# Four graph layers on one core: where the second chunk of layer 2 is fetched to, and where the pieces of layer 3 stand between the pairs

## The chip, the cores and the metric

The kernel runs on one core of a Trainium2 chip. A core has a matrix engine (TensorE, "PE" in the profile, with a row "PEld" for its weight loads), a vector engine (DVE), a scalar engine (ACT), GpSimd (POOL) and a sync engine (SP), which here only issues DMAs. The engines run side by side; each works off its own queue in order, and semaphores hold an instruction until what it needs is there. Matmuls write to PSUM, everything else lies in SBUF, and 16 DMA engines bring data from HBM.

The metric is device time in microseconds of one execution. Before the change, three executions took 528.18, 528.65 and 530.54 us; the median is 528.65.

## The reference

There are N = 3327 nodes with 64 features and a sparse N x N adjacency matrix. Four layers follow each other, each inside a residual with a layer norm:

```python
x = _layernorm(x + _L0_gnn_ref(x, adj, L0_gnn_W), axis=-1)
x = _layernorm(x + _L1_gnn_ref(x, adj, L1_gnn_weight, L1_gnn_bias), axis=-1)
x = _layernorm(x + _L2_gnn_ref(x, adj, L2_gnn_W, L2_gnn_b), axis=-1)
x = _layernorm(x + _L3_gnn_ref(x, adj, L3_gnn_weight, L3_gnn_bias), axis=-1)
```

The change concerns the last two. Layer 2 takes the sum over neighbours and a small dense step:

```python
h_neigh = (adj @ X + X) / deg
z = concat([X, h_neigh]) @ W + b
out = relu(z);  out / max(norm(out), 1e-12)
```

Layer 3 does not use the values of the adjacency but the place of each neighbour in its row, counted from the end, and weighs the last hundred with powers of one half:

```python
mask = (adj != 0)
rank = cumsum(mask, axis=1)
pos = rank - (deg - min(deg, 100))
w = mask * where(pos > 0, 0.5 ** (min(deg, 100) - pos), 0)
out = w @ (input @ weight) + bias
```

## The kernel before

**Tiling.** The nodes are padded to 3328 = 26 blocks of 128. The adjacency, transposed, is cut into 4 chunks of 832 target nodes (`CH`), and each chunk into 13 pairs of source blocks; one pair is 128 partitions x 2 x 832 fp32 (832 KB) and is fetched by `load_adj` (line 276) as one DMA, or as two when its target is a list of two tiles (line 281; the whole form is line 285). All these DMAs are issued by SP, in order.

**Layer 2** runs over the chunks in the order `ORDER2` = 2, 3, 1, 0. I call these pass 1 to pass 4. For a pair, `aggregate_pair` (line 442) issues four matmuls that add to the chunk's PSUM bank; the profile shows each as two instructions, so a pair is eight matmuls of line 448. After the last pair, `keep_sums` (line 432) copies the bank to SBUF in two halves (DVE or ACT, line 435), `prologue2` (line 1189, after the eleventh pair) has transposed the chunk's own features (line 1196), and `epilogue2` (line 1211) does the dense step and the norm: two matmul instructions per block on line 1218, then a chain on DVE, ACT and POOL from line 1224 to line 1259. Near its end the new features are split into three bf16 parts, high, middle and low (lines 1254 to 1257, tile `parts`), which layer 3 uses. The epilogue of pass 1 is issued behind the first pair of pass 2; that of pass 2 behind pass 2, and so on.

**Pass 2 also finds ranks.** The chunk 3 (`LATE_RANKS`) is the only one whose ranks are not yet known from layer 0. For each pair DVE makes a mask (line 474, or line 470 twice when the pair lies in two tiles), PE counts with twelve matmuls (`count`, line 520), DVE carries the count over to the next mask (`carry`, line 506), and ACT writes the ranks from PSUM to SBUF (line 530). The counts of a pair follow two pairs later (`LATE_LAG`). The ranks go to `last_rank`, which is the same memory as `uw`. The halves of `uw`, called `ut` and `wt`, are two operands of layer 1 that are no longer needed; each again has two halves, which hold one pair each. The one row of ranks that needs a correction is handled by `last_rows` (line 536) with small DMAs on POOL's queue and three DVE instructions (lines 548 to 550).

**Where pairs lie.** Most pairs go through four buffers (`adjp`). Since layer 1 needs them too, the first nine pairs of pass 1 are fetched during layer 1's end into memory that is free then (`load_ahead2`, line 1156): both halves of wt, both halves of ut (one of them twice) and eight tiles of layer 1 that hold half a pair each. The last four pairs of pass 1 are still in the four buffers from layer 1. Pairs 12 and 11 of pass 2, which come first there, go into four tiles of a pool with ten buffers (tag `m16`, line 1186), which the masks and the expanded ranks use as well:

```python
ahead = [
    load_adj(
        ORDER2[1], jp, [mp.tile([P, CH], FP, name="a1", tag="m16") for _ in range(2)]
    )
    for jp in (NB // 2 - 1, NB // 2 - 2)
]
```

**Layer 3** is cut into 52 pieces, one per pair and chunk. A piece needs the ranks of its pair and chunk, which `expand` (line 1265) turns into bf16 powers of two, nine pieces ahead, on DVE (line 1279) or ACT (line 1277), and the parts of the pair's two blocks. It is then twelve matmuls of line 1302 into a PSUM bank of its chunk. The four banks lie where the counts of pass 2 had theirs. Which part of `parts` exists when: pass 1's epilogue makes blocks 13 to 18, pass 2's 19 to 25. So a piece of pair 9 (blocks 18 and 19) and all of pairs 10 and 11 need pass 2's epilogue.

Twelve pieces (pairs 7, 8, 9) are issued in pass 3, one behind each pair from the second on; eight (pairs 10 and 11) in pass 4, one behind each pair from the first on; 32 after layer 2. In pass 3 the three pieces of chunk 3 come last (`sorted`, line 1351), since their ranks are the latest.

**The order.** The program is written with a framework that orders each engine's instructions itself, in the order of the program where it sees no reason against it. `issue_after(a, b)` (line 148) draws an edge without a semaphore: a stands behind b in the queue of their engine. In pass 2 every pair is pinned behind the counts before it in this way; in passes 3 and 4 neither pairs nor pieces are pinned, so their matmuls can be mixed.

Of the kernel before, what the change touches and what calls it, by code (L numbers as in the profile page):

```python
# [20 lines left out]
FP = mybir.dt.float32  # L21
# [10 lines left out]
P = 128  # L32
NB = 26
NP = NB * P
D = 64
CH = 832
# [6 lines left out]
ORDER2 = (2, 3, 1, 0)  # L43
# [67 lines left out]
def four_gnn_layers_kernel(  # L111
# [14 lines left out]
    nc = tc.nc  # L126
# [305 lines left out]
    def keep_sums(c, acc, row, both=False):  # L432

        for h in range(2):
            (nc.vector.tensor_copy if both and h == 0 else nc.scalar.copy)(
                sums[row : row + D, bass.ds(c * CH + h * HC, HC)], acc[h * D : (h + 1) * D, 0:HC]
            )

    def halves(t):
        return t.rearrange("p (h c) -> p h c", h=2)  # L440
# [200 lines left out]
    with ExitStack() as l0s:  # L641
# [3 lines left out]
        places = Places(banks)  # L645
# [507 lines left out]

    def load_ahead2(more):

        def load(k, t):  # L1160
            return load_adj(ORDER2[0], PAIRS[k], t)

        def view(t, k):
            return t[:, bass.ts(k, 2 * CH)].rearrange("p (b i) -> p b i", b=2)

        loaded = [load(k, view(*t)) for k, t in enumerate(((ut, 0), (wt, 0), (wt, 1)))]
        yield loaded
        places = [[more(2 * i + k) for k in range(2)] for i in range(4)]
        loaded += [load(3 + k, t) for k, t in enumerate((*places, view(ut, 1)))]
        yield  # L1170
        loaded.append(load(8, view(ut, 0)))

    def begin2(banks, loading, loaded, behind):

# [8 lines left out]
    def layers_2_and_3(banks, acc, done, there):  # L1183


        with tc.tile_pool(name="l2m", bufs=10) as mp, tc.tile_pool(name="late", bufs=1) as late:
# [24 lines left out]
            def epilogue2(c, x2, behind=None):  # L1211


                b0, b1_, nb = blocks_of(c, GROUPS2)
                work, alone = Work(nb), c == ORDER2[-1]
                pb = per_block(banks.pair(2), nb, 2 * D)
                for k in range(nb):
                    issued = nc.tensor.matmul(
                        pb[:, k, :], lhsT=sums[:, bass.ts(b0 + k, P)], rhs=wl2, start=True, stop=True
                    )  # L1220
                    if behind is not None:
                        issue_after(issued, behind)
                y = node_tile("y2")[:, 0:nb, :]
                nc.vector.tensor_tensor(y, pb[:, :, D : 2 * D], col(scale2[:, b0:b1_], nb), op=ALU.mult)
                nc.vector.tensor_tensor(y, y, pb[:, :, 0:D], op=ALU.add)
                nc.vector.tensor_scalar_max(y, y, 0.0)
                ss = work("ss")
                sum_of_squares(y, nb, ss, alone)

                m = small.tile([P, GB], FP, name="ln_m", tag="ln_m")  # L1230
                nc.vector.tensor_reduce(m[:, 0:nb], y, axis=AX.X, op=ALU.add)
                nc.vector.tensor_scalar(m[:, 0:nb], m[:, 0:nb], 1.0 / D, None, op0=ALU.mult)
                aside = nc.vector if alone else nc.gpsimd
                aside.tensor_tensor(y, y, col(m, nb), op=ALU.subtract)
                nc.vector.tensor_scalar_max(ss, ss, 1e-24)
                r, k = (rsqrt(ss, work), 1.0) if alone else (table_norm(ss, work), 0.375)
                nc.vector.scalar_tensor_tensor(y, y, k, col(r, nb), op0=ALU.mult, op1=ALU.mult)
                aside.tensor_add(y, y, x2)
                ss = work("ss")
                sum_of_squares(y, nb, ss, alone)  # L1240
                r, k = (deviation(ss, work), 1.0) if alone else (table_root(ss, work), -0.5 / D)
                left = node_tile("left")
                copy = nc.vector.tensor_copy if alone else nc.scalar.copy

                for k0, k1 in ((0, 3), (3, nb)) if alone else ((0, nb),):
                    xs = x3[:, b0 + k0 : b0 + k1, :]
                    first = nc.vector.scalar_tensor_tensor(
                        xs, y[:, k0:k1, :], k, col(r[:, k0:k1], k1 - k0), op0=ALU.mult, op1=ALU.mult
                    )
                    if k0 > 0:  # L1250
                        issue_after(first, issued)

                    hi, mid, lo = (parts[:, b0 + k0 : b0 + k1, bass.ts(i, D)] for i in range(3))
                    copy(hi, xs)
                    nc.vector.tensor_sub(left[:, k0:k1, :], xs, hi)
                    nc.vector.tensor_copy(mid, left[:, k0:k1, :])
                    issued = nc.vector.tensor_sub(lo, left[:, k0:k1, :], mid)
                xs = x3[:, b0:b1_, :]
                aside.tensor_tensor(
                    xs, xs, bias["b3"].to_broadcast([P, nb, D]), op=ALU.add  # L1260
                )

            acc3, begun, bits_of, ranks_of = {}, set(), {}, {}

# [16 lines left out]
                    issue_after(issued, behind)  # L1281
                return issued

            def piece(k):
                last = None
                if not acc3:

# [11 lines left out]
                for b in range(2):  # L1299
                    for part in range(3):  # L1300
                        for h in range(2):
# [4 lines left out]
                                start=(c not in begun and b == 0 and part == 0),  # L1306
                                stop=(last and b == 1 and part == 2),
                            )
                begun.add(c)
                return issued  # L1310

            def epilogue3(b0, b1_, bank, behind):
# [29 lines left out]
                if full < b1_:  # L1342
# [4 lines left out]

            early = {2: (7, 8, 9), 3: (10, 11)}
            pieces = [(c, jp) for jps in (*early.values(), (12, 4, 5, 6)) for jp in jps for c in ORDER2]
            behind = 4 * len(early[2])  # L1350
            pieces[0:behind] = sorted(pieces[0:behind], key=lambda piece: piece[0] == LATE_RANKS)
            pieces += [(c, jp) for c in ORDER2 for jp in (0, 1, 2, LAST_PAIR)]
            left3 = len(pieces) - 4 * NCH
            beside = range(left3 - L3_LEFT + BITS_AHEAD, left3 - L3_LEFT + BITS_AHEAD + L3_BESIDE)

            ahead = [
                load_adj(
                    ORDER2[1], jp, [mp.tile([P, CH], FP, name="a1", tag="m16") for _ in range(2)]
                )
                for jp in (NB // 2 - 1, NB // 2 - 2)  # L1360
            ]
            rows = last_rows(late, [(c, rank[:, c]) for c in ORDER2 if c != LATE_RANKS])
            next(rows)
            k = 0
            for n, c in enumerate(ORDER2):
                if n > 0:
                    acc = banks.one(n % 2)
# [7 lines left out]
                for i, jp in enumerate(order):  # L1375
                    if n == 0 and i < EARLY:
                        continue
                    if n == 0 and jp in there:
                        a2 = there.pop(jp)
                    elif n == 1 and i < 2:  # L1380
                        a2 = ahead.pop(0)
                    else:
                        a2 = load_adj(c, jp)
                    issued = aggregate_pair(acc, xr, a2, jp, i == 0, i == NB // 2 - 1, counted)
                    if n == 1 and i == 0:
                        epilogue2(ORDER2[0], x2, issued)
                    if ranks:
                        mask = ranks.mask(jp, a2)
                        counted = count(masked, places, min(LATE_LAG, jp), issued)
                    if i == OWN2_AT:  # L1390
                        x2, made = prologue2(c, issued)
                        if n == 0:
                            step(rows, made)
                            all_of(rows)
                    if n in early and 0 <= i - 3 + n < 4 * len(early[n]):
                        piece(k)
                        k += 1
                if ranks:
                    late_rows = last_rows(late, [(c, last_rank)])
                    next(late_rows)  # L1400
                keep_sums(c, acc, D, n > 0)

                if n > 0:
                    epilogue2(c, x2)
            while k < left3:
                piece(k)
                k += 1
# [73 lines left out]
```

## Time and profile before

| what | us |
|---|---|
| median of three executions | 528.65 |
| profiled execution, whole | 529.18 |
| its span in the profile | 527.5 |
| layers 0 and 1 and the change to layer 2, to the first pair of pass 1 | 349.8 |
| pass 1, to the first pair of pass 2 | 19.2 |
| pass 2, to the first pair of pass 3 | 36.2 |
| pass 3, to the first pair of pass 4 | 42.1 |
| pass 4, to the end of its epilogue's matmuls | 31.4 |
| the rest of layer 3 and the output | 48.9 |

The stages begin with the first line 448 matmul of the pass in PE's timeline (349.81, 368.95, 405.15, 447.22), and pass 4 ends with line 1218 at 478.60; the passes overlap, so the first pairs of pass 3 run between the last counts of pass 2.

In the profile every row is a group of instructions: the line, the engine, the operation, the tile that is written and those that are read. A bracket at the end of a timeline row gives how long the engine was idle just before, and what ended the wait. Matmuls overlap, so a row's duration is longer than its share of PE's time; the distance from start to start is what counts. A stretch row gives the busy time of each engine between two moments, the clock that PE was granted (1.00 is full), and the load on the DMA engines.

### The profile page before, as it was taken

What the parts mean: (1) busy time and instruction counts of PE and PEld (TensorE: products, weight loads), DVE (VectorE), ACT (ScalarE), POOL (GpSimd) and SP (SyncE); (2) the same over time, 40 slices, a digit from 0 to 9 for tenths busy, and PEclk for the clock granted to TensorE, in tenths of its full rate; (3) what the DMA queues carried; (4) which work ended last, traced back from release to release, by engine and by line L of the source; (5) the groups of instructions that cost most, each with busy time, mean ns of one, the idle gap of its engine ahead of it and who ended that gap; (6) DMA issues with size and microseconds to landing.
All of it is one profiled execution on the core that took longest, in us unless ns stands there. A gap on an engine that the chain in (4) does not pass through costs nothing.

```text
span 527.5 us, 8494 instructions
## 1 busy us (share of the span) xinstructions
PE 481.2 (91%) x3256; PEld 238.7 (45%) x3256; DVE 386.5 (73%) x704; ACT 334.9 (63%) x394; POOL 177.2 (34%) x150
## 2 busy tenths in 40 slices
PE   5999898999967999999998999899899998999993
PEld 3555343454432333533343344354444664656672
DVE  3565438979669978799789968976888973726844
ACT  1445544776868999879978896711477653316931
POOL 2001101212007788867876795503202120200000
PEclk9999999999999999999999999999999999999998
DMA  8899999989438687767767786397997796880012
GB/s 270 309 357 344 390 341 388 334 274 316 190 113 336 201 267 254 255 197 254 262 195 238 232 277 232 135 386 240 342 317 270 272 341 260 294 290 2 1 23 50
DMA packets 46179, 132.52 MB, mean 251 GB/s; under 512 B 6934, under 2 KB 7038, under 8 KB 46066
## 3 DMA queue, kind: packets, MB, share of 16 engines
q1 hardware_dynamic: 45602, 131.35, 72.3%
q0 software_dynamic: 384, 0.52, 0.4%
q8 instruction: 27, 0.44, 0.3%
q14 instruction: 22, 0.18, 0.1%
q10 hardware_dynamic: 144, 0.03, 0.0%
HBM read 130.86 MB, written 0.85 MB: 250 GB/s over the span
## 4 chain that ended last, share of the span: by engine, by line
PE 50%; DVE 23%; DMA 11%; ACT 10%; issue 3%; POOL 1%; DVEq 0%; ACTq 0%; POOLq 0%
PE one L448 13%; DMA adj<-in_adjt_dram 11%; PE two L1302 10%; DVE p L828 7%; PE two L817 6%; PE one L848 6%; PE two L520 5%; DVE mask L506 4%; PE two L448 4%; ACT s L841 3%; DVE s L836 3%; DVE mask L474 3%; ACT s L842 2%; ACT rank L530 2%; PE one L1317 1%
## 5 line engine op out<-in xcount | busy, mean ns | idle before, releaser
L843 POOL TENSOR_TENSOR s<-s,p 128x832 f32<-128x832 f32 x67 | 130.0, 1954 | 71.5 <-ACT s L842 59.5
L828 DVE SCALAR_TENSOR_TENSOR p<-two,adj 128x832 f32<-128x832 f32 x100 | 101.0, 1018 | 17.9 <-issue 13.4
L817 PE MATMUL two<-uw 64*128 64x416 f32 x416 | 88.5, 537 | 14.7 <-DVE s L836 7.1
L530 ACT ACTIVATE rank<-two,last_bias 128x832 uint8<-128x832 f32 x78 | 71.7, 952 | 46.3 <-PE two L520 24.3
L448 PE MATMUL one<-adj,x0w 128*64 128x416 f32 x416 | 82.6, 524 | 4.1 <-DMA adj<-in_adjt_dram 2.6
L848 PE MATMUL one<-s,xu 128*64 128x416 f32 x416 | 85.2, 524 | 0.0
L841 ACT ACTIVATE s<-two,far_bias 128x832 f32<-128x832 f32 x67 | 63.6, 950 | 21.9 <-DVE p L828 19.9
L506 DVE SCALAR_TENSOR_TENSOR mask<-two,minus_last,mask 32x832 bf16<-32x832 f32 x48 | 52.5, 1093 | 27.5 <-PE two L520 23.3
L448 PE MATMUL one<-adj,xr 128*64 128x416 f32 x296 | 69.7, 515 | 2.2 <-DMA adj<-in_adjt_dram 2.1
L1302 PE MATMUL two<-bits,parts 128*64 128x416 bf16 x624 | 69.0, 340 | 0.0
L817 PEld LDWEIGHTS two<-uw 64*128 64x128 f32 x416 | 36.8, 185 | 66.6 <-PE one L848 22.6
L474 DVE TENSOR_SCALAR mask<-adj 128x1664 bf16<-128x1664 f32 x50 | 52.7, 1055 | 15.5 <-DMA adj<-in_adjt_dram 14.6
L842 ACT ACTIVATE s<-s 128x832 f32<-128x832 f32 x67 | 60.1, 897 | 1.9
L520 PE MATMUL two<-mask,tri 128*64 128x416 bf16 x416 | 50.6, 345 | 10.1 <-DVE mask L506 7.6
L1302 PEld LDWEIGHTS <-parts 128*64 128x64 bf16 x624 | 40.2, 110 | 21.3 <-issue 3.4
L848 PEld LDWEIGHTS one<-s,xu 128*64 128x64 f32 x416 | 25.8, 136 | 47.5 <-issue 46.6
L448 PEld LDWEIGHTS one<-adj,x0w 128*64 128x64 f32 x416 | 29.2, 138 | 36.4 <-issue 23.4
L520 PEld LDWEIGHTS <-tri 128*64 128x64 bf16 x416 | 23.9, 110 | 44.2 <-issue 25.1
L836 DVE SCALAR_TENSOR_TENSOR s<-two,p 128x832 f32<-128x832 f32 x37 | 37.6, 1016 | 2.9 <-ACT two L833 2.4
L448 PEld LDWEIGHTS one<-adj,xr 128*64 128x64 f32 x296 | 27.1, 137 | 22.7 <-issue 14.7
L833 ACT ACTIVATE two<-two,far_bias 128x832 f32<-128x832 f32 x37 | 34.0, 918 | 4.9 <-DVE p L828 4.7
L1277 ACT ACTIVATE bits<-rank 128x1664 uint16<-128x1664 uint8 x21 | 32.3, 1579 | 5.6 <-PE two L1302 5.6
(265 smaller groups left out, 453.9 us busy)
## 6 DMA issues: line engine op xcount, KB each, us to landing
adj<-in_adjt_dram SPq DMA_DIRECT2D x139, 832.0 KB, 4.9
uw<-in_adjt_dram SPq DMA_DIRECT2D x5, 832.0 KB, 5.9
sums<-in_adjt_dram SPq DMA_DIRECT2D x2, 832.0 KB, 6.0
p<-in_adjt_dram SPq DMA_DIRECT2D x4, 416.0 KB, 5.1
s<-in_adjt_dram SPq DMA_DIRECT2D x4, 416.0 KB, 7.3
a<-in_adjt_dram SPq DMA_DIRECT2D x4, 416.0 KB, 4.0
uw<-in_xt_dram SPq DMA_DIRECT2D x1, 640.0 KB, 11.2
out_dram<-o SPq DMA_DIRECT2D x3, 192.0 KB, 2.5
```

Of the source, the lines that this page charges most:

```text
L448: issued = nc.tensor.matmul(acc[h * D : (h + 1) * D, 0:HC], lhsT=x[:, 2 * jp + k, 0:D], rhs=a[:, bass.ts(h, HC)], start=(first and k == 1) ...
L474: issued = nc.vector.tensor_scalar(mask, a2, 0.0, None, op0=ALU.not_equal)
L506: ranks.carried = nc.vector.scalar_tensor_tensor(halves(last), ranks.after[P - 32 : P, :, 0:HC], minus_last[P - 32 : P, :], halves(last), ...
L520: issued = nc.tensor.matmul(counts[k][rows, h, 0:HC], lhsT=lhsT[:, rows], rhs=mask[:, of, bass.ts(h, HC)], start=lhsT is tri, stop=(k == 1 ...
L530: nc.scalar.activation(halves(ranks.rank[:, 2 * jp + k, :]), counts[k][:, :, 0:HC], AF.Relu, bias=last_bias,)
L817: issued = nc.tensor.matmul(v[:, h, 0:HC], lhsT=wt[rows, bass.ts(jb, P)], rhs=ut[rows, bass.ds(c * CH + h * HC, HC)], start=True, stop=True,)
L828: issued = nc.vector.scalar_tensor_tensor(halves(p), v, 0.25 - 0.5 * FD, halves(a), op0=ALU.add, op1=ALU.mult)
L841: nc.scalar.activation(halves(s), v, AF.Square, bias=far_bias, scale=-2.0)
L842: nc.scalar.activation(s, s, AF.Copy, bias=FG)
L843: nc.gpsimd.tensor_mul(s, s, p)
L848: issued = nc.tensor.matmul(acc[h * D : (h + 1) * D, 0:HC], lhsT=xu[:, jb, 0:D], rhs=s[:, bass.ts(h, HC)], start=first, stop=last,)
L1302: issued = nc.tensor.matmul(acc3[c][h * D : (h + 1) * D, 0:HC], lhsT=parts[:, 2 * jp + b, bass.ts(part, D)], rhs=bits[:, b, bass.ts(h, HC) ...
```

## The change

Four things change, all in layers 2 and 3; no instruction is added or removed.

- Pass 2's first four pairs are now all fetched ahead. Pairs 12 and 11 go into the two halves of wt, pairs 10 and 9 into the four `m16` tiles. The other nine go through the four buffers.
- Each piece that is issued in passes 3 and 4 is pinned: its matmuls stand behind the last matmul of the pair before it, and the next pair's matmuls stand behind the piece.
- The sort covers all 20 pieces of passes 3 and 4 rather than the first 12. So the five pieces of chunk 3 come last of all, in pass 4, and three pieces of pair 10 move from pass 4 to pass 3.
- The first copy of a pass's sums (`keep_sums`, on DVE) stands behind the last parts instruction of the epilogue before it.

```diff
@@ keep_sums
         for h in range(2):
-            (nc.vector.tensor_copy if both and h == 0 else nc.scalar.copy)(
+            issued = (nc.vector.tensor_copy if both and h == 0 else nc.scalar.copy)(
                 sums[row : row + D, bass.ds(c * CH + h * HC, HC)], acc[h * D : (h + 1) * D, 0:HC]
             )
+            if h == 0:
+                first = issued
+        return first
...
+    def half_of(t, k):
+        return t[:, bass.ts(k, 2 * CH)].rearrange("p (b i) -> p b i", b=2)
...
@@ piece
-            def piece(k):
+            def piece(k, behind=None):
...
+                            if behind is not None:
+                                issue_after(issued, behind)
...
@@ layers_2_and_3
             early = {2: (7, 8, 9), 3: (10, 11)}
-            behind = 4 * len(early[2])
+            behind = 4 * sum(map(len, early.values()))
             pieces[0:behind] = sorted(pieces[0:behind], key=lambda piece: piece[0] == LATE_RANKS)
...
-            ahead = [
-                load_adj(
-                    ORDER2[1], jp, [mp.tile([P, CH], FP, name="a1", tag="m16") for _ in range(2)]
-                )
-                for jp in (NB // 2 - 1, NB // 2 - 2)
+            ahead = [half_of(wt, k) for k in range(2)] + [
+                [mp.tile([P, CH], FP, name="a1", tag="m16") for _ in range(2)] for _ in range(2)
             ]
+            ahead = [load_adj(ORDER2[1], NB // 2 - 1 - k, t) for k, t in enumerate(ahead)]
...
-                    elif n == 1 and i < 2:
+                    elif n == 1 and ahead:
                         a2 = ahead.pop(0)
...
                     if n == 1 and i == 0:
-                        epilogue2(ORDER2[0], x2, issued)
+                        made = epilogue2(ORDER2[0], x2, issued)
...
                     if n in early and 0 <= i - 3 + n < 4 * len(early[n]):
-                        piece(k)
+                        counted = piece(k, issued)
                         k += 1
...
-                keep_sums(c, acc, D, n > 0)
+                copied = keep_sums(c, acc, D, n > 0)
+                if made is not None and n > 0:
+                    issue_after(copied, made)

                 if n > 0:
-                    epilogue2(c, x2)
+                    made = epilogue2(c, x2)
```

## The prediction

> **What bounds the kernel now.** I read the page first, then the chain of waits, then a table of stretches, and last the timelines of PE, DVE and SP around the places where the chain leaves PE. "Pass 1" to "pass 4" are layer 2's four chunks in their order 2, 3, 1, 0. From the page and the chain in order of time:
>
> ```profile
> PE 481.2 (91%) x3256; PEld 238.7 (45%) x3256; DVE 386.5 (73%) x704; ACT 334.9 (63%) x394; POOL 177.2 (34%) x150
> ...
> 385.57 1.06 PE two L520 x12
> 386.63 1.40 PE one L448 x8
> ...
> 478.60 22.80 PE two L1302 x257
> ```
>
> PE is busy 91% of the span, and the chain gives clean prices: one pair of layer 2 (line 448) costs 1.40 us, the counts of one pair (line 520) 1.06, a matmul of layer 3 (line 1302) 22.80/257 = 0.0887, so a piece of twelve 1.065. Shares cannot tell what the change is worth; these stretches can (columns: PE, PEld, DVE, ACT, POOL busy, PE's granted clock, DMA share, GB/s):
>
> ```profile
> 357.00:360.00 3.00, 3.00 (x22) 1.16 (x17) 2.17 (x7) 0.54 (x1) 0.06 (x1) 1.00 0.32 121
> 368.95:405.15 36.20, 33.26 (x249) 16.68 (x247) 31.35 (x47) 23.65 (x29) 6.38 (x9) 1.00 0.95 326
> 377.80:380.05 2.25, 0.00 (x0) 0.00 (x0) 2.17 (x5) 1.99 (x4) 1.15 (x2) 1.00 0.97 163
> 415.49:449.05 33.56, 31.85 (x254) 18.97 (x255) 21.57 (x40) 14.01 (x15) 5.73 (x5) 1.00 0.77 277
> 444.00:449.00 5.00, 5.00 (x48) 3.13 (x43) 3.24 (x6) 3.25 (x3) 0.00 (x0) 1.00 0.06 22
> ```
>
> The DMA engines are nearly idle twice: at 357 to 360, where SP has nothing that it may issue, and at 444 to 449, where all four buffers are full and PE does not free one. Pass 2 (368.95 to about 405) loses PE time. PE, and then DVE:
>
> ```profile
> 377.28 0.52 PE L520 MATMUL two<-mask,tri 128*64 128x416 bf16 x4
> 380.05 0.54 PE L520 MATMUL two<-mask,tri 128*64 128x416 bf16 x4 [2.25 <-DVE mask L506]
> ...
> 383.28 0.54 PE L520 MATMUL two<-mask,tri 128*64 128x416 bf16 x4 [0.59 <-DVE mask L506]
> ```
> ```profile
> 374.22 1.03 DVE L474 TENSOR_SCALAR mask<-adj 128x1664 bf16<-128x1664 f32 x1 [0.74 <-DMA adj<-in_adjt_dram]
> ...
> 377.19 1.02 DVE L474 TENSOR_SCALAR mask<-adj 128x1664 bf16<-128x1664 f32 x1
> ...
> 378.91 1.09 DVE L506 SCALAR_TENSOR_TENSOR mask<-two,minus_last,mask 32x832 bf16<-32x832 f32 x1
> 380.40 1.03 DVE L474 TENSOR_SCALAR mask<-adj 128x1664 bf16<-128x1664 f32 x1 [0.41 <-DMA adj<-in_adjt_dram]
> ```
>
> PE waits 2.25 and 0.59 us for the carry (line 506), which stands in DVE's queue behind masks whose pairs landed late. Pass 3 ends like this:
>
> ```profile
> 439.61 0.56 PE L448 MATMUL one<-adj,xr 128*64 128x416 f32 x1 [1.22 <-DMA adj<-in_adjt_dram]
> ...
> 441.22 4.76 PE L1302 MATMUL two<-bits,parts 128*64 128x416 bf16 x52
> ```
> ```profile
> 432.83 0.61 DVE L1256 CAST parts<-left 128x448 bf16<-128x448 f32 x1
> 438.44 0.58 DVE L435 COPY sums<-one 64x416 f32<-64x416 f32 x1 [5.00 <-PE one L448]
> 439.06 0.62 DVE L1257 TENSOR_TENSOR parts<-left,parts 128x448 bf16<-128x448 f32 x1
> ```
>
> Pairs without pieces outran the DMA (0.30, 0.19 and 1.22 us of waits), then 52 piece matmuls ran in one block before pass 4's pairs, which is when the DMA idled. They needed the parts of line 1257, which DVE did only after a copy that waits for the pass's end.
>
> **The first edit: four pairs ahead.** Pairs 12 and 11 of pass 2 go to the two halves of wt, pairs 10 and 9 to the four tiles that held 12 and 11. Issues stay 15 (2 whole, 4 halves, 9 whole, against 4 halves and 11 whole), each 0.37 us of SP's free time. Before, SP stood here:
>
> ```profile
> SPq L281 <- PE two L448: 4.6, 1, 4.6
> ```
>
> until 359.90. The halves of wt come free when pass 1's pairs 1 and 2 are done (352.83 and 354.23), so the two loads can go at about 352.9 and 354.3, ahead of the halves that still wait. At the 406 GB/s of 352 to 356 they are 4.2 us of DMA work, of which the idle stretch takes about 3. Each later pair of pass 2 then has two pairs fewer ahead of it: the load behind the 0.41 us gap landed at 380.38 and would land near 375.
>
> Gain: the carry at 378.91 has in front of it the 0.74 us gap and the 1.02 us mask, both of which move ahead, so it starts 1.76 us earlier; its input (counts that ended at 376.05) allows that. The 0.59 us wait goes too, since the gap and mask before it at 380.40 move ahead. 1.76 + 0.59 = 2.35 us. Ends: 2.84 (both waits whole), and nothing, or up to 1.5 us lost, if DVE's line 548, which waits for POOL's small loads issued at 360.67 to 363.85 (6.6 and 7.0 us to land), is pushed back by the deeper DMA backlog; all masks queue behind it. I take 2.35. What is late next in pass 2 is PE itself: pair and counts are 2.46 us, DVE's mask and carry 2.12, a loaded pair 2.41 (852 kB at the 353 GB/s of 388 to 392).
>
> **The second edit: pins and order, costed together.** Pass 3's first two pairs stay free; from its third on, every pair stands behind a piece. That takes from PE the pairs which filled the end of pass 2's counts (1.75 pairs, 405.15 to 415.49 had no idle). I count from the counts' last matmul (412.40) to pass 4's second pair (449.05): 36.65 us before. After, the last counts start 0.4 earlier (their carry ended at 411.09; a pair held PE until 411.53): 412.0. Behind it stand epilogue2 twice (1.80 as at 476.80, and 1.61 as at 370.44), 13 pieces (13.85), 12 pairs (16.80), one prologue (0.85): 34.9 us, so 446.9, which is 2.15 less than 449.05, plus new waits:
>
> - The first piece needs the PSUM pairs that the counts used. ACT empties them by 415.13, while PE is through epilogue2 at 413.8: 1.35 us at most; ACT does 1.58 us of bits in between, without which it is nothing. I take the middle, 0.65.
> - The seventh piece (pair 9) is the first to need the second chunk's parts. PE gets to its second half at 413.8 + 0.65 + six pieces 6.4 + six pairs 8.4 + 0.5 = 429.8. The parts end 24.1 us after epilogue2's matmuls before (415.56 to 439.68), 18.5 without the copy in front (the new edge between copy and epilogue excludes it), and 16.2 if also the late ranks' bits are gone from that stretch (0.46 + 1.02 us at 427.41, 0.74 on ACT at 429.57, 0.5 at 430.86; they move to pass 4). So 432.3 or 430.0: a wait of 2.5 or 0.2. I take 0.5, nearer the second, since those bits do move.
>
> Moving the late pieces behind all others changes no count (20 pieces in passes 3 and 4, 32 after); pass 4 runs a piece behind each of its first eight pairs either way, and its tail stays paced by loads that wait for a buffer. At 2.465 us for pair and piece against 2.41 for a load, DMA keeps up; if it moved only the 326 GB/s of pass 2's row (2.61 us a pair), eleven pairs would cost 1.6 us more. The edge between copy and epilogue in pass 2 changes nothing: the copy stood at 408.94, the epilogue's end at 407.14.
>
> [...] Where PE stood idle 2.25 us at 377.80, the granted clock stayed 1.00. [...]
>
> **Sum.** -2.35 - 2.15 + 0.65 + 0.50 = -3.35 us. The profiled execution took 529.18 (span 527.5), 0.53 above the median 528.65. On the execution 525.83, on the median 525.3. A measurement tells about 0.5%, 2.6 us, from no change.
>
> **Rivals.**
> - *Both waits vanish.* -2.84 - 2.15, and the 0.7 us that PE idles at 402.3 to 403.3 for the first epilogue's DVE work: -5.7, 522.95. For it: pass 2's inputs land 5 us early. Against: DVE is 31.35 of 36.20 us busy there.
> - *The loads were not the limit.* If DVE's order of masks, epilogue and carry stays, pass 2 gains nothing: -1.0, 527.65. The same if the two loads wait for all of uw (in use until 362.6) and not for a half. Against: the load issued at 351.47 went as soon as its own half was free.
> - *Slower: pinned pieces wait for parts.* Place: the seventh to ninth piece. DVE's expansions of bits wait for pieces to free buffers (3.3 us in pass 3, longest 3.0), and the parts can queue behind them. Before, PE went on with pairs; pinned, it stands, and SP with it. The sum without this wait is -3.85, so it decides from 3.85 us on. Three expansions fall in that stretch; a period late (2.47) each they make 0.5 + 7.4 = 7.9: +4.05, 532.7; only two of them late, 530.2.
>
> **How the numbers follow.** Forecast 0.40, its own range 523.9 (-2.84 - 2.15 + 0 + 0.2) to 528.0 (-2.35 - 2.15 + 1.35 + 2.5); about 0.25 of it lies below 526.0, 0.15 within. Both vanish 0.25, all faster. Loads not the limit 0.13, all within. Slower 0.22: 0.14 beyond 531.3, 0.08 within. Faster 0.50, same 0.36, slower 0.14. The range 521.8 to 530.8 leaves out about 0.04 below and 0.15 above.
>
> **What would show it.** Right: SP issues two uw loads near 353 and 354; no DMA-idle stretch at 357; PE's gap before line 520 in pass 2 under 0.6 us; no block of 52 piece matmuls and no idle DMA at the end of pass 3; the late pieces all in pass 4; PE idle under 1.4 us before the first piece and under 2.5 at the seventh. Wrong: the carry still late with masks on time (second rival), a PE gap over 3.85 us before line 1302 in pass 3 released by line 1257 (third), or a lower clock behind it.

## The result: slower by 1.1%, and the profile after

The changed kernel took 535.12 us (median of 8 executions, 532.73 to 539.03), the kernel before 530.12 in the same comparison (8, 525.87 to 531.38): ratio 1.0106, 95% interval 1.0067 to 1.0145. The forecast was faster, 525.3, and its range ended at 530.8. All ratios and mean clocks here and below are of fast executions; that leaves out one slow execution, 531.90 of the run with pins in pass 4 only, which its median still holds.

The added lines move the numbers: pairs are now line 451, masks 473 and 477, the carry 509, counts 523, the row fix 551 to 553, `epilogue2` 1221, bits 1281 and 1283, parts 1257 to 1260, pieces 1306. The profiled execution took 535.87, its span 534.1. From start to start, in PE's timeline ("last counts" stands for 0.25 us before their last matmul ends, at 412.40 and 418.13; the second pair of pass 4 begins at 449.05 and 458.00):

| stretch | before, us | after, us |
|---|---|---|
| start to the first pair of pass 1 | 349.81 | 350.59 |
| pass 1 | 19.13 | 20.63 |
| pass 2, first five pairs | 15.06 | 17.85 |
| from there to the last counts | 28.14 | 28.82 |
| last counts to the end of the sixth piece | 14.40 | 16.67 |
| the next twelve piece matmuls (after: the seventh piece) | 5.25 | 5.96 |
| from there to the second pair of pass 4 | 17.25 | 17.49 |
| from there to the last matmul of the last `epilogue2` | 29.27 | 27.72 |
| the rest | 49.19 | 48.37 |

Pass 4 does not begin at 447.22 in the profile before: two of the eight matmuls of its first pair run at 439.61 and 440.01, ahead of the block of 52 piece matmuls. The table counts to the second pair for this reason.

The page's busy times, and from the chain of waits its longest piece:

```profile
PE 484.3 (91%) x3256; PEld 234.7 (44%) x3256; DVE 387.5 (73%) x704; ACT 335.5 (63%) x394; POOL 183.2 (34%) x150
```
```profile
486.00 22.80 PE two L1306 x257
```

PE is busy 3.1 us longer in a span 6.6 us longer. The last 257 piece matmuls take 22.80 us as before; what differs lies ahead of them. Stretches of after (PE, PEld, DVE, ACT, POOL busy, PE's clock, DMA share, GB/s):

```profile
357.00:360.00 3.00, 3.00 (x20) 1.26 (x18) 1.99 (x5) 0.74 (x2) 0.00 (x0) 1.00 1.02 397
...
381.20:384.20 3.00, 0.01 (x2) 0.01 (x2) 2.84 (x7) 1.50 (x3) 1.67 (x3) 1.00 0.04 8
384.30:387.70 3.40, 3.40 (x16) 1.51 (x17) 2.93 (x5) 3.37 (x5) 0.14 (x1) 0.51 0.10 30
...
434.00:441.00 7.00, 4.04 (x34) 1.77 (x30) 5.55 (x12) 1.55 (x5) 1.04 (x1) 1.00 0.91 325
```

The first edit does what it says: where the DMA engines stood at a share of 0.32, they are at 1.02 (357 to 360). Yet in pass 2 there is a stretch in which PE does nothing and the DMA next to nothing (381.20 to 384.20), and behind it 3.4 us at a clock of 0.51. At 434 to 441, PE is busy 4.04 of 7 us. The timelines name both places. PE and DVE in pass 2:

```profile
380.58 0.54 PE L523 MATMUL two<-mask,tri 128*64 128x416 bf16 x4 [0.87 <-DVE y L1228]
384.19 0.78 PE L523 MATMUL two<-mask,tri 128*64 128x416 bf16 x4 [3.07 <-DVE mask L509]
...
385.46 2.72 PE L451 MATMUL one<-adj,xr 128*64 128x416 f32 x8
```
```profile
373.52 0.59 DVE L551 TENSOR_SCALAR last_a<-last_a 78x832 f32<-78x832 f32 x1 [8.47 <-DMA adj<-in_adjt_dram]
...
375.15 1.01 DVE L477 TENSOR_SCALAR mask<-uw 128x1664 bf16<-128x1664 f32 x1
...
376.58 1.02 DVE L477 TENSOR_SCALAR mask<-uw 128x1664 bf16<-128x1664 f32 x1
...
383.05 1.09 DVE L509 SCALAR_TENSOR_TENSOR mask<-two,minus_last,mask 32x832 bf16<-32x832 f32 x1
```

DVE stands 8.47 us ahead of the row fix (line 551). The fix reads POOL's small loads; the last two of them were issued at 365.12 and 365.62 and landed at 373.25 and 373.44 (the profile puts the wait down to another load). Behind it stand the masks of pass 2's first two pairs, whose loads into the halves of wt (in the profile `uw`) had landed at 362.19 and 364.76. Before, the last two of these pairs' four half masks went at 367.58 and 369.69 and line 548 at 370.22: the fix stood behind them. Why the framework wrote the other order here is not shown. The carry (line 509) that PE waits for now runs 11.83 us behind the pass's first pair (383.05 against 371.22), 9.96 before (378.91 against 368.95); PE stands for 3.07 us, and the next pair takes 2.55 us from start to start instead of 1.40. PE in pass 3:

```profile
417.24 0.54 PE L523 MATMUL two<-mask,tri 128*64 128x416 bf16 x4 [0.90 <-ACT uw L533]
...
419.66 1.80 PE L1221 MATMUL two<-wl,sums 128*128 128x128 f32 x14 [1.52 <-ACT uw L533]
...
436.12 0.69 PE L1306 MATMUL two<-bits,parts 128*64 128x416 bf16 x6
438.25 0.37 PE L1306 MATMUL two<-bits,parts 128*64 128x416 bf16 x2 [1.43 <-ACT parts L1257]
439.56 0.37 PE L1306 MATMUL two<-bits,parts 128*64 128x416 bf16 x2 [0.95 <-DVE parts L1259]
440.51 0.37 PE L1306 MATMUL two<-bits,parts 128*64 128x416 bf16 x2 [0.58 <-DVE parts L1260]
```

Three waits in a row inside the seventh piece, 1.43 + 0.95 + 0.58 us, for three steps of the parts; and 0.90 + 1.52 us ahead of the epilogue at the end of the counts, where before a pair of pass 3 ran. The rest of the second edit is there as announced: a piece between two pairs, no block of 52 matmuls, and pass 4 from its second pair on is 1.55 us shorter.

### The profile page after: what moved, and what is told of

It is laid out like the page before. It is cut to its first block, busy times and chain, and to the rows that moved or that the text cites. A ratio compares the mean times of both kernels' runs of the same rounds, so it can differ in the third digit from the quotient of the medians.

```text
span 534.1 us, 8497 instructions
## 1 busy us (share of the span) xinstructions
PE 484.3 (91%) x3256; PEld 234.7 (44%) x3256; DVE 387.5 (73%) x704; ACT 335.5 (63%) x394; POOL 183.2 (34%) x150
## 4 chain that ended last, share of the span: by engine, by line
PE 46%; DVE 26%; ACT 11%; DMA 6%; issue 6%; POOL 2%; POOLq 0%; DVEq 0%; ACTq 0%
PE one L451 12%; PE two L1306 9%; DVE p L831 7%; PE two L820 7%; DMA adj<-in_adjt_dram 6%; PE one L851 6%; DVE mask L509 4%; PE two L523 4%; DVE s L839 3%; DVE mask L477 3%; ACT s L844 3%; PE two L451 3%; ACT s L845 2%; ACT rank L533 2%; PE two L888 1%
## 5 line engine op out<-in xcount | busy, mean ns | idle before, releaser
L831 DVE SCALAR_TENSOR_TENSOR p<-two,adj 128x832 f32<-128x832 f32 x100 | 101.1, 1019 | 17.8 <-issue 13.3
L820 PE MATMUL two<-uw 64*128 64x416 f32 x416 | 90.2, 548 | 13.6 <-DVE s L839 7.2
L1306 PE MATMUL two<-bits,parts 128*64 128x416 bf16 x624 | 59.9, 340 | 3.0 <-ACT parts L1257 1.4
L477 DVE TENSOR_SCALAR mask<-adj 128x1664 bf16<-128x1664 f32 x48 | 50.9, 1061 | 13.6 <-DMA adj<-in_adjt_dram 12.9
L451 PE MATMUL one<-adj,xr 128*64 128x416 f32 x280 | 56.6, 523 | 0.0
L1306 PEld LDWEIGHTS <-parts 128*64 128x64 bf16 x624 | 35.1, 110 | 29.0 <-issue 8.6
L533 ACT ACTIVATE uw<-two,last_bias 128x832 uint8<-128x832 f32 x26 | 24.3, 951 | 7.8 <-DVE mask L509 6.9
```

Source lines behind the costliest of these rows:

```text
L451: issued = nc.tensor.matmul(acc[h * D : (h + 1) * D, 0:HC], lhsT=x[:, 2 * jp + k, 0:D], rhs=a[:, bass.ts(h, HC)], start=(first and k == 1) ...
L477: issued = nc.vector.tensor_scalar(mask, a2, 0.0, None, op0=ALU.not_equal)
L533: nc.scalar.activation(halves(ranks.rank[:, 2 * jp + k, :]), counts[k][:, :, 0:HC], AF.Relu, bias=last_bias,)
L820: issued = nc.tensor.matmul(v[:, h, 0:HC], lhsT=wt[rows, bass.ts(jb, P)], rhs=ut[rows, bass.ds(c * CH + h * HC, HC)], start=True, stop=True,)
L831: issued = nc.vector.scalar_tensor_tensor(halves(p), v, 0.25 - 0.5 * FD, halves(a), op0=ALU.add, op1=ALU.mult)
L1306: issued = nc.tensor.matmul(acc3[c][h * D : (h + 1) * D, 0:HC], lhsT=parts[:, 2 * jp + b, bass.ts(part, D)], rhs=bits[:, b, bass.ts(h, HC) ...
```

## The experiments

Theories. *The row fix*: the first edit gives its 2.35 us only if DVE's masks stay ahead of the row fix. *Waits that pairs used to fill*: the pins of pass 3 cost what PE waits at the end of the counts and in the seventh piece. Rivals: the sort and the edge cost by themselves, the pins of pass 4 cost, or the loss is spread over all pinned pieces.

**The two edits apart.** The first alone: the fetch of after, with before's sort, no pins, no edge between copy and parts.

```diff
-            behind = 4 * sum(map(len, early.values()))
+            behind = 4 * len(early[2])
...
-                        counted = piece(k, issued)
+                        piece(k)
...
-                if made is not None and n > 0:
-                    issue_after(copied, made)
```

> Before, with only the first edit: pass 2's pairs 12 and 11 go to wt, 10 and 9 to the four small tiles; no pins, the old sort, no edge. My theory now: the loss of the change has three places, and the first of them is made by this edit alone. DVE's queue has the row fix (line 551), which waits for POOL's small loads, ahead of the first masks of pass 2, so masks that have long landed wait for it, and PE waits for the carry before the fifth pair. Expected: PE idle before that pair 3 to 4 us (2.84 before), the masks of pairs 12 and 11 not before line 551, and 2 to 4 us slower than before, 532 to 534, a short half-clock stretch after the wait included. Rival of my prediction: the edit gains its 2.35 us and the pins alone lose, 527.8. Rival of the clock: half-clock stretches fall anywhere and the edits cost nothing, within 1 us of before.

Measured 528.81 beside 527.94: ratio 1.0023 [0.9998, 1.0048]. The second alone: after with the old fetch.

```diff
-            ahead = [half_of(wt, k) for k in range(2)] + [
-                [mp.tile([P, CH], FP, name="a1", tag="m16") for _ in range(2)] for _ in range(2)
-            ]
-            ahead = [load_adj(ORDER2[1], NB // 2 - 1 - k, t) for k, t in enumerate(ahead)]
+            ahead = [
+                load_adj(
+                    ORDER2[1], jp, [mp.tile([P, CH], FP, name="a1", tag="m16") for _ in range(2)]
+                )
+                for jp in (NB // 2 - 1, NB // 2 - 2)
+            ]
```

> Before, with all but the first edit: pieces pinned, late pieces last, the edge; pairs 12 and 11 in the small tiles as before. My theory: pass 2 is as before (2.25 and 0.59 us of waits); PE idles about 1.7 us before epilogue2 and the first piece of pass 3 (ACT has not emptied the counts' PSUM) and about 3.5 us inside the seventh piece (parts of the second chunk not ready); against that no block of 52 piece matmuls and a pass 4 that is 1.5 us shorter. Together 1 to 3 us slower than before, 531 to 533. If the prediction's sum for this edit held, 1 us faster; by the clock rival no change.

Measured 532.65 beside 527.94: 1.0100 [1.0065, 1.0134]. So nearly all of the loss is the second edit's; the first alone neither gains nor loses much, where I had expected it to lose 2 to 4 (532 to 534). DVE and PE of the first edit alone show why it does not gain:

```profile
369.94 0.59 DVE L551 TENSOR_SCALAR last_a<-last_a 78x832 f32<-78x832 f32 x1 [4.76 <-DMA a<-in_adjt_dram]
...
371.56 1.02 DVE L477 TENSOR_SCALAR mask<-uw 128x1664 bf16<-128x1664 f32 x1
...
373.00 1.02 DVE L477 TENSOR_SCALAR mask<-uw 128x1664 bf16<-128x1664 f32 x1
```
```profile
380.62 0.54 PE L523 MATMUL two<-mask,tri 128*64 128x416 bf16 x4 [1.92 <-DVE mask L509]
...
383.97 0.54 PE L523 MATMUL two<-mask,tri 128*64 128x416 bf16 x4 [0.53 <-ACT uw L533]
```

The order is that of after, masks behind the fix; PE's waits of 1.92 and 0.53 us take the place of 2.25 and 0.59 before. In after the fix came 2.30 us behind pass 2's first pair (373.52 against 371.22), here 0.09 us (369.94 against 369.85); the wait in pass 2 stayed under 2 us, and no half clock (a granted clock of 0.50) followed: the eight count matmuls and the pair behind it took 0.73 and 1.39 us from start to start, 0.73 and 1.40 before. In the third run with this fetch and this place of the fix (the late start, below) it came 1.69 us behind, and PE waited 3.07 us again.

**The row fix moved behind the third mask of pass 2**, first in after, then in the first edit alone:

```diff
                         mask = ranks.mask(jp, a2)
+                        if i == 2:
+                            step(rows, mask)
+                            all_of(rows)
...
                         if n == 0:
-                            step(rows, based)
-                            all_of(rows)
+                            pass
```

> After, with one thing moved: the row fix (lines 551 to 553) is issued behind the third pair's mask in pass 2. Nothing is left out. My theory: this takes away the block in DVE's queue; the masks of pairs 12 and 11 run at about 363 to 366 when they land, PE's wait before the fifth pair falls from 3.9 us to under 1, no half-clock stretch follows it, and the whole is 4 to 5.5 us faster than after: about 530, no slower than before by more than 1 us. If it is the deeper DMA backlog that delays the masks and not their place in the queue, the wait stays at 3 to 4 us and the time at 535.

> The first edit alone (four pairs ahead, no pins, old sort), with the fix of the last row issued behind the third pair's mask of pass 2 rather than in pass 1. Theory: the fetch gives what the forecast said, as soon as DVE's masks no longer stand behind the fix that waits for POOL's small loads. The first edit alone came to 528.8 beside 527.9 of the kernel before; p13 to p18 shrinks from 14.65 us to about 12.4, so 525.0 to 526.5. Rival: the gain of the moved fix (3.8 us beside pins) was pass 3's waits falling at another moment; without pins nothing is left of it, 528 to 529.

(In the second expectation p13 to p18 are pass 2's first five pairs.) In after: 528.82 beside 527.94, 1.0025 [0.9996, 1.0054], against 1.0106 with the fix where it was. In the first edit alone: 525.31 beside 528.01, 0.9957 [0.9929, 0.9985]; it gains 2.7 us. PE's and DVE's rows of the latter, to be set beside those above:

```profile
366.03 0.59 DVE L473 TENSOR_SCALAR mask<-a 128x832 bf16<-128x832 f32 x1
367.76 0.59 DVE L473 TENSOR_SCALAR mask<-a 128x832 bf16<-128x832 f32 x1 [1.14 <-DMA a<-in_adjt_dram]
369.22 0.59 DVE L551 TENSOR_SCALAR last_a<-last_a 78x832 f32<-78x832 f32 x1 [0.87 <-DMA last_a<-in_adjt_dram]
```
```profile
380.64 0.51 PE L523 MATMUL two<-mask,minus 128*64 128x416 bf16 x3 [0.43 <-DVE mask L509]
...
385.97 0.54 PE L523 MATMUL two<-mask,tri 128*64 128x416 bf16 x4 [0.24 <-DVE mask L509]
```

Masks first, then line 551. PE waits 0.43 and 0.24 us where it waited 2.25 and 0.59. From pass 2's first pair to the last counts it is 40.30 us against 43.20 before. One profile of before is not the whole of it: the old fetch stands in seven kernels whose first five pairs of pass 2 are the same, and there PE's long wait is 1.23 to 2.86 us and the five pairs take 14.23 to 15.29 us. With the fix moved they take 12.43 us in all three kernels that have it (here, in after, and in the last run below), and PE waits 0.43 us. The forecast's mechanism holds; its price is not paid in the changed kernel because of the order in one queue.

**Pass 3's pieces from the fourth pair on**, ten in pass 3 and ten in pass 4:

```diff
-                    if n in early and 0 <= i - 3 + n < 4 * len(early[n]):
+                    if n in early and 0 <= i - 3 * (3 - n) < (10 if n == 2 else 10):
```

> After, with the pieces of pass 3 behind its fourth to thirteenth pair (ten) instead of its second to thirteenth (twelve), and ten in pass 4 instead of eight. Nothing is left out. My theory: the third and fourth pair fill the time in which ACT empties the counts' PSUM, and the seventh piece comes 2.8 us later, when the parts are nearly there; PE's idle time before the first piece falls from 2.8 us to under 0.5 and inside the seventh piece from 3.5 us to under 1; pass 2 keeps its wait of 3 to 4 us. 3.5 to 5 us faster than after: 530 to 531.5. If the pins cost nothing, no change: 535.

Measured 533.67 beside 527.94, 1.0098 [1.0063, 1.0133], not the 530 to 531.5 expected. The first wait went (3.33 us from the last counts to the first piece, as before), the seventh piece's did not: PE stands 4.38 us ahead of a pair inside it, and the profile names a load, which landed at 438.90; the parts ended at 438.34. Which of the two held it is not told apart. At 437.0 a stretch of 6.8 us at half clock begins.

**The second edit taken to pieces**, all on the old fetch, each diff against the second edit alone: without any pins (sort and edge stay); pins in pass 4 only; all pins, but six pieces in pass 3 and thirteen in pass 4.

```diff
-                        counted = piece(k, issued)
+                        piece(k)
```

> The second edit without its pins: the sort over 20 pieces and the edge between the copy and the epilogue's parts, on the old fetch. Whole, the second edit came to 532.65 beside 527.9. Theory (pieces that wait hold PE): without pins PE goes on with pairs while a piece waits, so 527 to 528.5. Rival (the order itself costs: the copy of the sums behind the parts keeps the bank, the late pieces crowd pass 4): 531 or more here too.

```diff
-                        counted = piece(k, issued)
+                        if n == 3:
+                            counted = piece(k, issued)
+                        else:
+                            piece(k)
```

> As the one without pins, but the eight pieces of pass 4 are pinned between its pairs. Theory (the pins of pass 3 cost, at the first and the seventh piece): 526.5 to 528.5, with the 1.5 us that the end of pass 4 was shorter with pins. Rival (the pins of pass 4 cost, since a pair that waits for its load now also holds the piece): 530.5 or more.

```diff
-                    if n in early and 0 <= i - 3 + n < 4 * len(early[n]):
+                    if n in early and 0 <= i - 3 + n < (6 if n == 2 else 13):
```

> The second edit whole on the old fetch, pins in both passes, but only six pieces in pass 3 (pairs 7 and 8, which need no parts of the second chunk); thirteen in pass 4. Theory (the seventh piece waits for the parts, 3.5 us with PE idle, and the clock halves behind it): the wait is gone and the median falls by 3 to 4 us against the 532.65 of the whole edit, to 528.5 to 529.7; the first piece's wait of about 1.5 us remains. Rival (the loss is spread: no pairs at the end of the counts, the first piece's wait and the pass 4 loads): 531.5 or more, since the seventh piece is only one place of it.

Beside 528.01: without pins 527.12, 0.9980 [0.9958, 1.0003]; pins in pass 4 only 525.89, 0.9951 [0.9924, 0.9978]; six in pass 3 531.68, 1.0058 [1.0029, 1.0087]. So the sort and the edge together cost nothing (neither was run alone), and with the pins of pass 4 added they still cost nothing; the pins of pass 3 do, 6.8 us from 525.89 to 532.65 by the medians and 7.9 by the ratios (1.0100 against 0.9951). The profiles of the first two differ, from pass 1's first pair to the end of pass 4, by more than 0.1 us only in pass 2's first pairs (14.65 and 14.24), ahead of all pins and within the spread above; that pass 4's pins gain by themselves is not shown.

The third came to what its rival had named, 531.5 or more, though by a wait that neither had named. The wait for the parts is gone, the 1.52 us ahead of the epilogue stay, but six pairs then follow each other without a piece and outrun the loads:

```profile
428.99 5.75 PE L451 MATMUL one<-adj,xr 128*64 128x416 f32 x32
...
439.90 2.33 PE L451 MATMUL one<-adj,xr 128*64 128x416 f32 x8 [2.79 <-DMA adj<-in_adjt_dram]
```
```profile
440.70:447.50 6.80, 6.03 (x20) 3.17 (x16) 0.58 (x1) 0.50 (x1) 0.00 (x0) 0.50 0.83 315
```

A wait of 2.79 us for a load, and 6.8 us at a clock of 0.50 behind it, took the place of the wait for the parts.

PE of pass 4's pins alone, and then of the second edit whole (each granted a clock of 1.00 from 398 to 447), from the last counts on:

```profile
409.73 1.56 PE L451 MATMUL one<-adj,xr 128*64 128x416 f32 x8
411.23 1.83 PE L1221 MATMUL two<-wl,sums 128*128 128x128 f32 x14
...
435.55 3.86 PE L1306 MATMUL two<-bits,parts 128*64 128x416 bf16 x41
```
```profile
410.19 0.54 PE L523 MATMUL two<-mask,minus 128*64 128x416 bf16 x4
412.25 1.80 PE L1221 MATMUL two<-wl,sums 128*128 128x128 f32 x14 [1.52 <-ACT uw L533]
...
431.19 0.37 PE L1306 MATMUL two<-bits,parts 128*64 128x416 bf16 x2 [1.79 <-ACT parts L1257]
432.51 0.37 PE L1306 MATMUL two<-bits,parts 128*64 128x416 bf16 x2 [0.95 <-DVE parts L1259]
433.45 0.37 PE L1306 MATMUL two<-bits,parts 128*64 128x416 bf16 x2 [0.58 <-DVE parts L1260]
```

Without pins in pass 3, the order that the framework wrote has a pair (409.73) between the last counts and the epilogue, and it fills the time until the parts are complete (435.36) with pairs, with twelve matmuls behind the first six pieces (as many as the first halves of two pieces of pair 9, which need no new parts), and with four more as each of the first two parts arrives (433.16 and 434.48); 41 piece matmuls follow in a block (435.55). PE does not wait from the last counts to that block. So a block like that of before, which I had taken for a loss, is where the late parts are waited out. With pins nothing may stand there: 1.52, and 1.79 + 0.95 + 0.58 = 3.32 us of waits. From the last counts to the second pair of pass 4 it is 40.46 us with the pins of pass 3 and 35.60 without: 4.86 more, and the four waits are 4.84. The two profiled executions, 528.46 and 523.20, are 5.26 us apart.

**First six or last six of pass 3's pieces pinned** (pass 4 pinned, old fetch; diffs against pins in pass 4 only):

```diff
-                        if n == 3:
+                        if n == 3 or k < 6:
```

> The second edit on the old fetch, where in pass 3 only the first six pieces are pinned (and the eight of pass 4). Without pins in pass 3 it was 525.9, with all twelve 532.65. Theory: the cost is two waits of PE that pairs filled before, 1.52 us ahead of the epilogue at the end of the counts and 3.3 us in the seventh piece; here the first alone, and the pieces behind the sixth let pairs pass: 527 to 528. Rival (the pins cost at each piece, or by pairs that outrun their loads later): 529 or more.

```diff
-                        if n == 3:
+                        if n == 3 or k >= 6:
```

> The same with only the last six pieces of pass 3 pinned (pairs 9; pair 10 of the three early chunks) and the eight of pass 4. Theory: the wait of the seventh piece for the parts alone, some 3.3 us, and a stretch at half clock behind it in some executions: 529 to 530.5. Rival (the six free pieces run ahead of the pairs as before, so the seventh piece comes earlier and waits longer): 531 or more. Rival (the wait is harmless, its time is made up where the loads wait later): 526 to 527.5.

Beside 527.86: first six 527.99, 1.0008 [0.9984, 1.0032]; last six 532.08, 1.0078 [1.0050, 1.0107]. Against pass 4's pins alone (525.89) that is 2.1 us by the medians and 3.0 by the ratios, not clear of the wait of 1.52 at intervals of about 1.3 us to either side; and 6.2 or 6.7 us, where 3.1 to 4.6 had been expected. What is missing stands in the profile of the last six:

```profile
433.23 0.37 PE L1306 MATMUL two<-bits,parts 128*64 128x416 bf16 x2 [3.53 <-ACT parts L1257]
434.54 0.56 PE L1306 MATMUL two<-bits,parts 128*64 128x416 bf16 x2 [0.95 <-DVE parts L1259]
435.49 0.56 PE L1306 MATMUL two<-bits,parts 128*64 128x416 bf16 x2 [0.38 <-DVE parts L1260]
435.83 2.98 PE L451 MATMUL one<-adj,xr 128*64 128x416 f32 x8
438.61 2.29 PE L1306 MATMUL two<-bits,parts 128*64 128x416 bf16 x12
```
```profile
434.30:441.10 6.80, 6.17 (x26) 2.58 (x28) 1.26 (x3) 1.59 (x1) 0.65 (x1) 0.50 0.17 35
```

The free pieces run ahead, so the seventh comes earlier (PE stops 13.3 us after the epilogue's matmuls, 15.4 in the second edit whole) and waits longer (3.53 + 0.95 + 0.38 = 4.86 us), and 6.8 us at half clock follow: the pair and the piece behind take 2.78 and 2.08 us from start to start instead of 1.40 and 1.06. The rival that the six free pieces run ahead was right.

**Both mended in one**: after with the fix behind the third mask and no pins in pass 3.

```diff
                         mask = ranks.mask(jp, a2)
+                        if i == 2:
+                            step(rows, mask)
+                            all_of(rows)
...
                         if n == 0:
-                            step(rows, based)
-                            all_of(rows)
+                            pass
...
-                        counted = piece(k, issued)
+                        if n == 3:
+                            counted = piece(k, issued)
+                        else:
+                            piece(k)
```

> The changed kernel with two of its steps mended: the fix of the last row behind the third mask of pass 2, and no pins in pass 3 (the eight pieces of pass 4 stay pinned, sort and edge stay). Theory: the two gains lie in different stages and add. The fetch with the fix moved gave 525.3 beside 528.0, the second edit without the pins of pass 3 gave 525.9: 522.7 to 524. Rival (one gain is taken back by the other, since an earlier end of pass 2 only makes pass 3 wait longer for its loads): 525 to 526.

Measured 524.45 beside 527.86: 0.9921 [0.9889, 0.9953], faster than both kernels by the interval. The two gains, 2.7 and 2.1, would add to 4.8; 3.4 was measured, and the interval holds both the sum and a gain partly taken back.

## Why the prediction was wrong

**The fetch, -2.35.** The mechanism was right, the step that failed is "the 0.74 us gap and the 1.02 us mask, both of which move ahead": it took DVE's order as given and moved only the landings. With four pairs ahead, the masks of `uw`'s pairs stand behind the fix, which waits for POOL's small loads. The prediction had named line 548 and "all masks queue behind it", as an end of its range for a later landing. What decided was where the fix stands: +0.9 us alone, -2.7 once moved. The profile of after accounts for the place: PE's waits of 0.87 and 3.07 us and the half clock's 1.69 (below) in place of 2.25 and 0.59 make 2.79 us, which is what the first five pairs took longer.

**The path of pass 3, -2.15.** The sum of 34.9 us without waits was near: the second edit alone spends 40.46 with 4.84 of waits, so 35.6. But the step that failed is that the gain was put down to the pins. Without pins in pass 3 the same path is 35.60, and in the two runs of the first edit alone, which have neither pins nor the new sort nor the edge, it is 35.38 and 35.72; the pins only add their waits. In before it was 36.90, with 0.30 + 0.19 + 1.22 = 1.71 us of PE's waits for loads in it; where it is 35.60 there are none, and the two runs of the first edit have 0.96 and 0.50. Those waits are more than the 1.30 us between 36.90 and 35.60, so that what the sort and the edge earn by themselves is not shown. "That takes from PE the pairs which filled the end of pass 2's counts" stood in the text, and no price beside it.

**The first piece, +0.65.** Measured 0.90 + 1.52 in after, 0.18 + 1.52 in the second edit alone. "PE is through epilogue2 at 413.8" failed: the epilogue's PSUM tile is itself one that ACT must empty (line 533), so that the epilogue waits, not the piece behind it.

**The seventh piece, +0.50.** Measured 2.96 in after, 3.32 in the second edit alone, beyond the upper end of 2.5. The step that failed is that the parts end 16.2 us after the epilogue's matmuls, since the late ranks' bits leave the stretch (the times listed for these bits add up to 2.72 us, which would make it 15.8). They ended 19.0 us after (421.46 to 440.46), near the 18.5 given for the case in which only the copy goes. The copy did go from the front, but bits are expanded nine pieces ahead, and with fifteen early pieces the first late one is expanded beside the seventh. DVE in after:

```profile
427.37 1.01 DVE L1283 TENSOR_SCALAR bits<-rank 128x1664 uint16<-128x1664 uint8 x1
...
428.81 1.01 DVE L1283 TENSOR_SCALAR bits<-rank 128x1664 uint16<-128x1664 uint8 x1
...
430.76 1.02 DVE L1283 TENSOR_SCALAR bits<-rank 128x1664 uint16<-128x1664 uint8 x1
...
435.44 1.02 DVE L1283 TENSOR_SCALAR bits<-uw 128x1664 uint16<-128x1664 uint8 x1
```

The fourth row reads `uw`, a late rank. The first three now stand in the middle of the norm, between the sums at 425.24 and the product at 432.16 (6.9 us; 4.2 before, 419.34 to 423.58, without bits there). From those sums to the last part DVE did four expansions before (427.41, 429.49, 430.42, 431.89) and does four now, so that no bits left the stretch. This is the third rival's mechanism, expansions of bits ahead of the parts. Its place was right and its deciding point, 3.85 us, was not reached: the forecast fell by the other terms as well.

**The clock, for which the sum had no term.** Before, PE's 2.25 us wait was followed by a granted clock of 1.00 (380.05 to 384.00). In after, 3.07 us of waiting were followed by 3.4 us at 0.51, in which the eight count matmuls behind the wait and the next pair took 0.54 and 1.15 us longer (1.27 and 2.55 us from start to start, 0.73 and 1.40 before): 1.69. The prediction named a lower clock only behind a gap at the seventh piece. In after it came in pass 2, and at the seventh piece, with its 2.96 us of waits, the granted clock was 1.00 (434 to 441).

**The terms together.** First edit +0.9 where -2.35 was said; second edit +4.7 where -1.0 was said (-2.15 + 0.65 + 0.50). Their sum, +5.6, is near the measured +5.0. Of the second edit's loss against its version without pass 3's pins (6.8, or 7.9 by the ratios), 4.84 are the four waits. The rest may go with the clock: its mean over the executions was 0.9862 with the pins of pass 3 and 0.9915 without. That is 5.6 us more at half speed (0.0053 x 2 x 528), worth 2.8 us at the 1.69 us for 3.4 above; the two make 7.6. But that pins cause this part is not shown: the kernel before had 0.9875 and 0.9890 in the same two comparisons, and the one traced execution of the second edit alone (0.994) was granted 1.00 from 398 to 447, with all of pass 3's pieces in it. That pass 1 took 1.50 us more in after is a stretch at half clock (350.2 to 353.6); in the runs with both edits pass 1 took 20.78 with the fix moved, 19.13 with the late start and 19.14 in the last one, so I do not put it down to the change.

## What to carry to other kernels

When a load is moved earlier, look at who stands ahead of its consumer in that engine's own queue: here a three-instruction fix that waits for small loads cost the whole gain (528.81 us beside 527.94), and moving it gave the gain back (525.31 beside 528.01). A pin that makes an order even also forbids the fillers that an uneven order had found; price the wait that a filler covered before taking the filler away. Look at the granted clock behind a wait as well: 3.07 us of waiting cost PE another 1.69 us by 3.4 us at 0.51, while at the seventh piece, with 2.96 us of waits in three, the clock stayed 1.00.

## What the runs showed that I had not expected

The stretches at half clock that I saw ahead of the span's end were 3.4 us long (at 350.2 and 384.3 in after), 6.8 us, or about 10 us (159 to 169 in the last version, where the matmuls of lines 820 and 851 took up to 1.8 times as long as in before), and the length of one wait did not decide whether one came. One followed each of the waits of 2.79 us (six pieces in pass 3), 3.07 us (after) and 3.53 us (the last six pinned), and one began inside the wait of 4.38 us (the late start). None followed the unbroken wait of 2.86 us in pass 2 of the second edit alone (ended at 378.78; the mean clock of that execution, 0.994, makes 6.3 us at half speed in all, and before and after have about 5 and 6 at the span's end), nor the 3.32 us in its pass 3 and the 2.96 us in after, where four piece matmuls split the waiting in three (granted clock 1.00 from 428.7 to 441.0 and from 434 to 441). At about 150 to 166 us, in layer 1, where PE waits four times for 1.1 to 1.8 us, it came in some profiles and not in others of kernels that are the same there: none in before, 6.8 us at 152 in after. Why equal waits end differently no run here tested.
